# Moving the FFN's activation transposes from TensorE to SBUF transfers and VectorE block transposes

## The chip, the cores and the metric

The kernel runs on one core of a Trainium2 chip. The core has five engines that run side by side, each taking its own instructions in order: TensorE (PE; matrix products and transposes, results in PSUM), VectorE (DVE), ScalarE (ACT), GpSimd (POOL), and SyncE (SP), which here does nothing but issue transfers to the core's 16 DMA engines. They wait for one another by semaphores. The metric is the device time of one execution in microseconds (us); lower is better.

## What is computed

A transformer block in float32 over 2 x 1024 tokens of 1024 features: a layer norm, a convolution of width 3 that makes q, k and v, attention inside blocks of 128 tokens, two projections and a residual; then the part that matters here, an FFN with a gate over four experts:

```python
def ffn(x, ...):                                  # x: layer norm of the block's middle result
    y = einsum('bth,oh->bto', x, W_base) + b_base
    z = einsum('bth,erh->bter', x, lora_A[active])
    contribs = einsum('bter,eor->bteo', z, lora_B[active]) * 2.0
    logits = (einsum('bth,eh->bte', x, router_W) + router_b)[..., active]
    alpha = softmax(log(domain_prior[active] + 1e-12) + logits)
    return y + einsum('bteo,bte->bto', contribs, alpha)
x = x + attention(layernorm(x), ...)
x = x + ffn(layernorm(x), ...)
```

## The kernel before

**Stages.** The convolution runs first, then attention, then the FFN, which begins near 500 us and takes the rest. The FFN works on 16 tiles of 128 tokens, two tiles at a time: eight pairs, m = 0 to 7.

**One pair.** The product with W_base (1024 x 1024) is done in the Strassen-Winograd way. The pair's activations are a 2 x 2 grid of blocks, A11 and A12 for the first tile (features 0 to 511 and 512 to 1023), A21 and A22 for the second. From them come S1 = A21 + A22, S2 = S1 - A11, S3 = A11 - A21 and S4 = A12 - S2. Seven products of half size (`PRODUCTS`, line 1258) replace eight. Their order on TensorE is 1 (A11), 6 (S2), 2 (A12 with weight B21), 5 (S1), 7 (S3), 3 (S4 with weight B22), 4 (A22). For accuracy each operand is held as a high part (a rounding, made on ScalarE, `op_hi`, line 1248) and a low part (the rest, made on VectorE, `op_lo`, line 1251), and each product is three matmuls.

**Where the activations come from.** TensorE needs the features along the partitions, while the layer norm leaves the tokens there. For tile n: a load of the residual (`load_xr`, line 1169), an addition on GpSimd (`add_projb`, 1173), the attention's last projection on TensorE (`project`, 1176) and its addition (`residual`, 1187), statistics (`x_stats`, 1191), the reciprocal root on GpSimd (`x_rstd`, 1197) and the normalised tile on VectorE (`x_norm`, 1202). Then `transpose_x` (line 1208) transposes each half of the tile by four TensorE transposes of 128 x 128 into one PSUM bank. `op_hi`, `op_lo` and `sum_s` (line 1235) read that bank; A21 alone is first copied to SBUF by ScalarE (`keep_a21`, line 1232), since S1 and S3 would otherwise have two inputs in PSUM. `drop` (line 1254) frees a bank.

**Weights.** Four of the seven right-hand sides stay in SBUF, a fifth is kept too in pieces, and B21 and B22 are streamed in every pair as two loads of 1 MB each into the two `vh` buffers (`stream`, line 1634; `load_half`, line 1119). A `vh` buffer comes free when the product that read it has run: B22's halves take the buffers that product 2 has just read B21 from, and the next pair's B21 takes those of product 3.

**What sets the order.** A planner writes the order of every engine by hand before the program is built. Each piece of work is an `Op` (line 270) with an engine, an estimated time, a due time, the work it comes after and the buffers it takes (`need`) and returns (`give`). `trace` (line 293) simulates: when an engine is free, it takes, in order of due times, the first piece that is ready. What it writes down is an order; on the chip an engine then does its work in that order and waits for whatever is not yet there. DMA issues on SP are planned as one engine of this kind ("DMA"). Work with `port=True` is kept apart from GpSimd's work of the same kind. The buffer pool `a4` (11 buffers of 4 KB a partition) holds the normalised tiles, the operands and the sums; the pool `m` is the eight PSUM banks.

**The pair's loop** (line 1813): while pair m is multiplied, the two tiles of pair m+1 are projected, normalised and transposed: `plan_p(2m+3)`, product 1, `plan_p(2m+2)`, products 6 and 2, transposes of the second tile, product 5, the gate's small products (`z_products`), product 7, transposes of the first tile, products 3 and 4, with the gate's contributions (`experts`) in between. Pair 0's transposes lie before the loop.

Of the kernel before, what the change touches and what calls it, by code (L numbers as in the profile page):

```python
# [16 lines left out]
ALU = mybir.AluOpType  # L17
# [4 lines left out]
P = 128  # L22
# [17 lines left out]
def preln_block_kernel(  # L40
# [19 lines left out]
    nc = tc.nc  # L60
    N, L, D = x.shape
# [10 lines left out]
    E = lora_b.shape[0] // R  # L72
# [577 lines left out]
    DVE, ACT, PE, DMA = "DVE", "ACT", "PE", "DMA"  # L650
# [4 lines left out]
    loaded, gs, gone = {}, {}, {}  # L655
# [7 lines left out]
    at = [14.0]  # L663
# [3 lines left out]
    def turn(i, h):  # L667

        due = at[0]
        if h == 0:  # L670
            how = HOW[i]
            if how == "scalar":
                o = Op(ACT, 1.3, due - 8.0, 8.0, [loaded[i]], partial(ln_sum, i))
                o = Op(ACT, 1.2, due - 6.0, 8.0, [o], partial(ln_square, i))
                o = Op(DVE, 0.1, due - 4.5, 8.0, [o], partial(ln_variance, i), lag=1.8)
            else:
                lag = 1.0 if how == "vector" else 1.8
                o = Op(DVE, 1.6, due - 5.5, 8.0, [loaded[i]], partial(ln_stats, i), lag=lag)
# [52 lines left out]
    for q, (v, n, dc) in enumerate(units):  # L731
# [10 lines left out]
        o = Op(DVE, 1.28, due - 5.5, 9.0, took, partial(unit_sum, q))  # L742
        o = Op(ACT, 0.55, due - 3.5, 9.0, [o], partial(unit_hi, q))
        side = Op(DVE, 0.64, due - 1.5, 9.0, [o], partial(unit_lo, q))
        for i in range(2):
            d = dc + i
# [4 lines left out]
            for c in range(NCC):  # L751
                after = [last, side, ready[v, d]]
# [48 lines left out]
    for v, dc in [(v, dc) for v in (1, 2, 3) for dc in range(0, NDC, 2)] + [(4, 0), (4, 2)]:  # L801
        if (v, dc) == (2, 0):

            for r in range(4):
                load(
                    at[0] + r, 3.0, nc.sync.dma_start, mask[r::4], causal[ts(r, P // 4)],
                    after=[last],
# [4 lines left out]
        side = begin_step(v, dc, at[0])  # L812
# [18 lines left out]
    for c in range(NCC):  # L831
        got = load(
            at[0] - 4.0, 8.0, tokens_load, 0, c, t3, NV - 1,
            after=[gone["m", v, c] for v in (0, 5, 1, 2, 3)],
# [4 lines left out]
        o = Op(DVE, 2.7, at[0] + 1.0, 6.0, [got, gone[4, c]], partial(tokens_join, 0, c))  # L839
        o = Op(ACT, 0.6, at[0] + 4.0, 6.0, [o], partial(tokens_hi, 0, c))  # L840
# [23 lines left out]
    def a4(name, shape, dt=F32):  # L864
        return ap_.tile([P, *shape], dt, tag="a4", name=name, bufs=A4)
# [197 lines left out]
    NH = NDC // 2  # L1063
# [149 lines left out]
            xns.pop(g)  # L1213


    AT = {(0, 0): "A11", (0, 1): "A12", (1, 0): "A21", (1, 1): "A22"}

    def operand(m, n):
# [209 lines left out]
    gs = [ch * NB + b for ch in (2, 3, 0, 1) for b in range(NB)]  # L1428
    d = {}

    def pe(key, takes, after, f, lead=8.0, need=("m",), give=()):
        d[key] = Op(PE, takes, at[0], lead, [d.get(a) for a in after], f, need=need, give=give)
        at[0] += takes
        return d[key]

    def op(key, e, takes, due, after, f, lead=14.0, **kw):
        if e in (DVE, ACT):
            kw.setdefault("lag", LAG)
            takes *= ROOM
        d[key] = Op(e, takes, due, lead, [d[a] for a in after if a in d], f, **kw)  # L1440
        return d[key]
# [93 lines left out]
    def plan_p(n):  # L1535
        g = gs[n]
        ch = g // NB
        plan_x(n, at[0])

        if ch < NCHUNK - 2 and g % NB == 1:  # L1540
            for wc in range(NWC):
                op(("oh", ch, wc), DMA, 1.4, at[0] - 8.0, [("os", ch, wc)], partial(load_oh, ch, wc),
                   lag=3.0, need=("t4",), lead=6.0)
                d["ol", ch, wc] = d["oh", ch, wc]
        for h in range(2):
            pe(("P", n, h), MM,
               [("ol", ch, wc) for wc in range(NWC)] + [("rl", "pw", wc, h) for wc in range(NWC)],
               partial(project, g, h), give=("t4",) * 2 if h and g % NB == NB - 2 else ())
            op(("r", n, h, 0), DVE, 0.6, at[0] + 0.5, [("P", n, h), ("xb", n)],
               partial(residual, g, h), give=("m",))  # L1550
        op(("xs", n), DVE, 1.6, at[0] + 2.0, [("r", n, 0, 0), ("r", n, 1, 0)], partial(x_stats, g))
        op(("xp", n), POOL, 0.3, at[0] + 3.5, [("xs", n)], partial(x_rstd, g), lag=0.3)
        op(("xn", n), DVE, 0.75, at[0] + 5.0, [("xp", n)], partial(x_norm, g), need=("a4",), port=True)

    def plan_tx(m, t, h):

        n, o = 2 * m + t, AT[t, h]
        pe(("TX", n, h), 0.44, [("xn", n)], partial(transpose_x, gs[n], h), give=("a4",) if h else ())
        d["A", m, o] = d["TX", n, h]
        due = at[0]  # L1560

        def more(key, e, takes, dt, after, f, **kw):
# [12 lines left out]

        def done(n, dt, after):
            more(("x", n), DVE, 0.0, dt, after, partial(drop, m, n), give=("m",))

        def free(n, dt, after):
            more(("f", n), DVE, 0.0, dt, after, int, give=("a4",))  # L1580

        if {"A21", "A22"} <= made and ("s", m, "S1") not in d:
            more(("s", "S1"), DVE, 0.6, 1.9, [("c", "A21"), ("A", "A22")], partial(sum_s, m, "S1"))
            done("A22", 2.0, [("s", "S1"), ("l", "A22")])
            split("S1", 3.0, [])
        if {"A11", "A21", "A22"} <= made and ("s", m, "S2") not in d:
            more(("s", "S2"), DVE, 0.6, 2.6, [("s", "S1"), ("A", "A11")], partial(sum_s, m, "S2"),
                 need=("a4",))
            more(("s", "S3"), DVE, 0.6, 3.3, [("s", "S1"), ("A", "A11")], partial(sum_s, m, "S3"))
            done("A11", 3.4, [("s", "S2"), ("s", "S3"), ("l", "A11")])  # L1590
            split("S2", 4.0, [])
            split("S3", 6.0, [])
            free(0, 7.0, [("l", "S1"), ("l", "S3"), ("s", "S2")])
        if len(made) == 4:
            more(("s", "S4"), DVE, 0.6, 4.0, [("s", "S2"), ("A", "A12")], partial(sum_s, m, "S4"))
# [340 lines left out]
```

## Time and profile before

| | us |
|---|---|
| median of 3 runs | 753.68 (753.35 to 755.99) |
| the profiled execution, device time | 752.35 |
| its span in the profile | 750.5 |
| one pair in the loop, start to start | 30.3 |
| TensorE transposes `trx` (L1211), whole kernel, busy | 16.6, 128 of them |
| granted TensorE clock | 0.999 of full speed |

The span is the profiled execution without the 1.85 us around it. Busy time is counted per engine. A row of a group gives the line, engine, operation, what is written and read, the shape and the count, then the busy time, the mean time of one in ns, and the engine's idle time before it with what ended it. "PEq" or "SPq" is an engine's own queue: for SP, the row of a transfer is the time its issue holds SP, not the time the transfer takes.

The core's 16 DMA engines moved 149.46 MB in 65423 packets, 199 GB/s on the mean:

```profile
q1 hardware_dynamic: 61488, 138.51, 51.1%
```

That is the queue of SP: packets, MB and share of the 16 engines' span.

### The profile page before, as it was taken

How to read it: one execution, taken by the hardware profiler on the slowest of the kernel's cores; microseconds unless marked ns; L12 is line 12 of the kernel's file. 1: busy time of each engine (PE TensorE's matmuls, PEld its weight loads, DVE VectorE, ACT ScalarE, POOL GpSimd, SP SyncE). 2: the span in 40 equal slices, each digit the busy share in tenths (PEclk: the TensorE clock that was granted, in tenths of full speed). 3: DMA queues.
4: the chain of work that ended last, by engine and by line, in shares of the span. 5: the costliest groups of instructions: out<-in, count | busy, mean ns of one | idle time of the engine just before them, and what ended most of it. 6: DMA issues, size and time to landing. Idle time of an engine off the chain costs nothing.

```text
span 750.5 us, 12939 instructions
## 1 busy us (share of the span) xinstructions
PE 741.9 (99%) x4746; PEld 633.9 (84%) x4746; DVE 596.3 (79%) x1051; ACT 421.3 (56%) x1044; POOL 187.4 (25%) x154
## 2 busy tenths in 40 slices
PE   8999999999999999999999999999999999999997
PEld 7999988888888888888888888888888888888886
DVE  6888899889767898898888888599667677577752
ACT  6888336464745998798898789863212212212120
POOL 3224321310000223132222312454142251331401
PEclk9999999999999999999999999999999999999999
DMA  9936994995753113363245344797655566565644
GB/s 342 379 104 206 248 267 107 292 287 124 249 167 127 44 50 103 132 220 103 99 153 206 131 151 138 266 386 317 227 211 225 215 238 235 209 225 217 227 174 168
DMA packets 65423, 149.46 MB, mean 199 GB/s; under 512 B 5918, under 2 KB 25006, under 8 KB 60240
## 3 DMA queue, kind: packets, MB, share of 16 engines
q1 hardware_dynamic: 61488, 138.51, 51.1%
q0 software_dynamic: 3728, 10.00, 7.4%
q8 instruction: 37, 0.61, 0.3%
q14 instruction: 26, 0.21, 0.1%
q10 hardware_dynamic: 144, 0.13, 0.1%
HBM read 114.01 MB, written 34.60 MB: 198 GB/s over the span
## 4 chain that ended last, share of the span: by engine, by line
PE 95%; DVE 2%; DMA 1%; ACT 1%; SPq 1%; issue 0%; DVEq 0%; ACTq 0%
PE pm L141 27%; PE pq L141 11%; PE py_c L1271 6%; PE pw L141 6%; PE py_a L1271 6%; PE pp L141 6%; PE py_e L1271 6%; PE pv L141 5%; PE po L978 4%; PE s L914 4%; PE pt L961 4%; PE py_b L1271 3%; PE pz L1288 2%; PE trx L1211 2%; PE tr L393 1%; DMA xt<-in_x 1%
## 5 line engine op out<-in xcount | busy, mean ns | idle before, releaser
L141 PE MATMUL pm<-v,u 128*128 128x256 f32 (+1 forms) x1152 | 203.1, 337 | 1.2 <-ACT v L481 0.6
L141 PEld LDWEIGHTS pm<-v,u 128*128 128x128 f32 x1152 | 177.8, 189 | 24.0 <-ACT v L481 0.9
L954 POOL TENSOR_TENSOR p<-p,rs 128x1024 f32<-128x1024 f32 x32 | 60.7, 1908 | 250.4 <-DVE rs L950 240.5
L943 ACT ACTIVATE p<-p,nmx 128x128 f32<-128x128 f32 x256 | 99.7, 398 | 4.3 <-DVE nmx L938 4.1
L141 PE MATMUL pq<-yt,wqk 128*128 128x512 f32 x384 | 94.6, 398 | 0.0
L141 PEld LDWEIGHTS pq<-yt,wqk 128*128 128x128 f32 x384 | 70.3, 188 | 16.8 <-issue 1.9
L1174 POOL TENSOR_TENSOR xr<-xr,projb 128x1024 f32<-128x1024 f32 x16 | 38.8, 2426 | 113.2 <-DMA xr<-in_x 104.7
L943 ACT ACTIVATION_READ_ACCUMULATOR p<-p,nmx 128x1 f32 x256 | 50.2, 196 | 0.0
L929 DVE TENSOR_TENSOR p<-s,mask 128x512 f32<-128x512 f32 x64 | 42.4, 685 | 9.7 <-PE s L914 9.5
L141 PE MATMUL pw<-oT,wot 128*128 128x512 f32 x192 | 47.9, 397 | 0.0
L141 PE MATMUL pv<-wvt,yt 128*128 128x512 f32 x192 | 47.1, 395 | 0.0
L141 PEld LDWEIGHTS pv<-wvt,yt 128*128 128x128 f32 x192 | 36.0, 188 | 8.8
L141 PEld LDWEIGHTS pw<-oT,wot 128*128 128x128 f32 x192 | 35.9, 188 | 8.7 <-DVE oT L999 0.2
L431 POOL DMA_DIRECT2D g<-in_conv_w x24 | 21.3, 938 | 69.9 <-ACT g L427 36.2
L453 DVE TENSOR_TENSOR u<-g,u 128x768 fp32r<-128x768 f32 x40 | 37.5, 953 | 1.5 <-ACT u L449 1.4
L969 DVE COPY pT<-pt 128x512 f32<-128x512 f32 x32 | 21.8, 688 | 20.8 <-PE pt L961 20.8
L938 DVE TENSOR_REDUCE nmx<-p 128x8 f32<-128x1024 f32 x32 | 37.7, 1196 | 0.1
L1233 ACT COPY s<-trx 128x512 f32<-128x512 f32 x8 | 4.7, 588 | 56.9 <-PE trx L1211 56.9
L449 ACT CAST u<-g 128x768 fp32r<-128x768 f32 x40 | 32.7, 838 | 5.2 <-PE pm L141 4.8
L914 PEld LDWEIGHTS s<-qk,qk 64*128 64x128 f32 x512 | 30.1, 187 | 5.1 <-issue 2.3
L914 PE MATMUL s<-qk,qk 64*128 64x128 f32 x512 | 34.0, 280 | 0.0
L1369 ACT COPY u<-py_a 128x512 f32<-128x512 f32 x8 | 4.7, 588 | 51.9 <-PE py_a L1271 51.9
(206 smaller groups left out, 1532.6 us busy)
## 6 DMA issues: line engine op xcount, KB each, us to landing
wb_B<-wsd_B SPq DMA_DIRECT2D x32, 1024.0 KB, 7.1
g<-in_conv_w SPq DMA_DIRECT2D x48, 384.0 KB, 8.3
mdr<-m SPq DMA_DIRECT2D x36, 256.0 KB, 3.0
g<-in_conv_w POOLq DMA_DIRECT2D x24, 384.0 KB, 7.3
xt<-in_x SPq DMA_DIRECT2D x16, 512.0 KB, 9.8
xr<-in_x SPq DMA_DIRECT2D x16, 512.0 KB, 5.6
out<-xr SPq DMA_DIRECT2D x14, 512.0 KB, 6.5
ml<-mdr SPq DMA_DIRECT2D x18, 384.0 KB, 4.0
```

What stands on the lines that cost most here:

```text
L141: nc.tensor.matmul(ps, l[a], r[b], start=first and i == 0, stop=last and i == 2)
L449: nc.scalar.copy(us[v, dc][0], raws[v, dc])
L453: nc.vector.tensor_tensor(lo, raws.pop((v, dc)), hi, ALU.subtract)
L914: nc.tensor.matmul(s[j][:, b, :], qh[ts(j, DH), ts(b, P)], kh[ts(j, DH), ts(b, P)], start=True, stop=True,)
L929: nc.vector.tensor_tensor(ps[i][0][:, ts(j, NB), :], ss[i][j], mask[:, None, :].to_broadcast([P, NB, P]), ALU.add,)
L938: nc.vector.tensor_reduce(nmx, p, AX.X, ALU.max, negate=True)
L943: nc.scalar.activation(p[:, k, :], p[:, k, :], AF.Exp, bias=nmx[:, k : k + 1], accum_out=sm[:, k : k + 1],)
L954: nc.gpsimd.tensor_tensor(p, p, rs[:, :, None].to_broadcast([P, 2 * NB, P]), ALU.mult)
L961: nc.tensor.transpose(pt[:, ts(b, P)], ps[i][0][:, j * NB + b, :], ident)
L978: nc.tensor.matmul(po[ts(j, DH), ts(b, P)], vh[:, b, ds((i % 4) * P + j * DH, DH)], pT[:, j, ts(b, P)], start=True, stop=True,)
L1174: nc.gpsimd.tensor_tensor(xrs[g], xrs[g], pwt["b"], ALU.add)
L1271: nc.tensor.matmul(pys[m, b], l[x], r[y], start=opens and c == 0 and i == 0, stop=c == NH - 1 and i == 2, skip_group_check=not opens,)
```

## The change

For pairs 1 to 7, the transposes leave TensorE. A tile is instead rearranged in SBUF: `spread` issues 16 transfers on SP, in four groups (a = 0 to 3) of four (q = 0 to 3). Each moves, for 32 tokens and all eight chunks of 128 features, a run of 32 features (128 bytes) per chunk from the tokens' 32 partitions to partitions 32a to 32a+31. After it the tile consists of 32 x 32 blocks that each lie where they belong but are not transposed. `turn` transposes these blocks on VectorE, 128 x 512 elements in one instruction for each half of the tile, and writes them back into the normalised tile. The result therefore stands in SBUF and not in PSUM, so A21 needs no copy, the sums and low parts of these pairs read two SBUF inputs and are planned with `port=True`, and buffers of `a4` are held in place of PSUM banks. In the plan a group of four transfers costs 0.7 us of SP (`XD`), and its data is taken to be there 4.0 us after the group's end. The last product of the last pair also gets two further conditions for its order. Pair 0 keeps its transposes on TensorE.

```diff
+    QB = P // 32
+    xps = {}
+
+    def spread(g, a):
+        if a == 0:
+            xps[g] = a4(f"xp_{g}", (D,))
+        src = xns[g].rearrange("p (c a f) -> p c a f", a=QB, f=32)
+        dst = xps[g].rearrange("p (c q f) -> p c q f", q=QB, f=32)
+        for q in range(QB):
+            nc.sync.dma_start(dst[ts(a, 32), :, q], src[ts(q, 32), :, a])
+
+    def turn(g, h):
+
+        t = xns[g][:, ts(h, 512)]
+        nc.vector.transpose(t, xps[g][:, ts(h, 512)])
+        trxs[g, h] = t.rearrange("p (c j) -> p c j", c=NH)
+        if h == 1:
+            xns.pop(g)
+            xps.pop(g)
...
     def sum_s(m, n):
         g0, g1 = gs[2 * m : 2 * m + 2]
+        a21 = trxs[g1, 0] if (g1, 0) in trxs else s_of(m, "S3")
         a, b, how = {
-            "S1": (trxs.get((g1, 1)), s_of(m, "S3"), ALU.add),
+            "S1": (trxs.get((g1, 1)), a21, ALU.add),
             "S2": (s_of(m, "S1"), trxs.get((g0, 0)), ALU.subtract),
-            "S3": (trxs.get((g0, 0)), s_of(m, "S3"), ALU.subtract),
+            "S3": (trxs.get((g0, 0)), a21, ALU.subtract),
...
+    XD = 0.7
...
         op(("xn", n), DVE, 0.75, at[0] + 5.0, [("xp", n)], partial(x_norm, g), need=("a4",), port=True)
+        if n > 1:
+            for a in range(QB):
+                op(("xd", n, a), DMA, XD, at[0] + 2.5 + XD * a, [("xn", n), ("xd", n, 0)], partial(spread, g, a),
+                   lag=4.0 if a else 0.0, need=("a4",) if a == 0 else ())
...
-        pe(("TX", n, h), 0.44, [("xn", n)], partial(transpose_x, gs[n], h), give=("a4",) if h else ())
+        if m == 0:
+            pe(("TX", n, h), 0.44, [("xn", n)], partial(transpose_x, gs[n], h), give=("a4",) if h else ())
+        else:
+            op(("TX", n, h), DVE, 0.6, at[0] - 1.5 + 0.7 * h, [("xd", n, a) for a in range(QB)],
+               partial(turn, gs[n], h), give=("a4",) if h else ())
...
-        if o == "A21":
+        if o == "A21" and side:
+            d["c", m, o] = d["A", m, o]
+        elif o == "A21":
...
-            more(("l", o), DVE, 0.6, 1.2, [("h", o)], partial(op_lo, m, o))
+            more(("l", o), DVE, 0.6, 1.2, [("h", o)], partial(op_lo, m, o), port=side)
...
-            more(("s", "S3"), DVE, 0.6, 3.3, [("s", "S1"), ("A", "A11")], partial(sum_s, m, "S3"))
+            more(("s", "S3"), DVE, 0.6, 3.3, [("s", "S1"), ("A", "A11")], partial(sum_s, m, "S3"),
+                 port=side)
...
-        pe(("Y", m, 3, 1 + x), 6 * 0.12, [("wl", "B22", 1, m)], partial(multiply_last, m, x), need=())
+        pe(("Y", m, 3, 1 + x), 6 * 0.12, [("wl", "B22", 1, m), ("E", m, 0, 1), ("Y", m, 3, x)], partial(multiply_last, m, x), need=())
```

More of the change, by code (lines that the diff above doesn't have):

```diff
@@ L1553, in plan_p @@
         op(("xn", n), DVE, 0.75, at[0] + 5.0, [("xp", n)], partial(x_norm, g), need=("a4",), port=True)
+        if n > 1:
+            for a in range(QB):
+                op(("xd", n, a), DMA, XD, at[0] + 2.5 + XD * a, [("xn", n), ("xd", n, 0)], partial(spread, g, a),
+                   lag=4.0 if a else 0.0, need=("a4",) if a == 0 else ())
     def plan_tx(m, t, h):
         n, o = 2 * m + t, AT[t, h]
-        pe(("TX", n, h), 0.44, [("xn", n)], partial(transpose_x, gs[n], h), give=("a4",) if h else ())
+        if m == 0:
[3 more added lines that the diff above has]
+               partial(turn, gs[n], h), give=("a4",) if h else ())
         d["A", m, o] = d["TX", n, h]
         due = at[0]
+        side = m > 0
         def more(key, e, takes, dt, after, f, **kw):
             op((key[0], m, *key[1:]), e, takes, due + dt, [(a[0], m, *a[1:]) for a in after], f, **kw)
-        if o == "A21":
+        if o == "A21" and side:
+            d["c", m, o] = d["A", m, o]
+        elif o == "A21":
             more(("c", o), ACT, 0.5, 0.5, [("A", o)], partial(keep_a21, m), need=("a4",), give=("m",))
@@ L1576, in done @@
         def done(n, dt, after):
-            more(("x", n), DVE, 0.0, dt, after, partial(drop, m, n), give=("m",))
+            both = ("x", m, {"A11": "A12", "A12": "A11"}.get(n)) in d
+            give = ("m",) if not side else ("a4",) if both else ()
+            more(("x", n), DVE, 0.0, dt, after, partial(drop, m, n), give=give)
         def free(n, dt, after):
@@ L1582, in plan_tx @@
         if {"A21", "A22"} <= made and ("s", m, "S1") not in d:
-            more(("s", "S1"), DVE, 0.6, 1.9, [("c", "A21"), ("A", "A22")], partial(sum_s, m, "S1"))
+            more(("s", "S1"), DVE, 0.6, 1.9, [("c", "A21"), ("A", "A22")], partial(sum_s, m, "S1"),
+                 need=("a4",) if side else (), port=side)
             done("A22", 2.0, [("s", "S1"), ("l", "A22")])
@@ L1587, in plan_tx @@
             more(("s", "S2"), DVE, 0.6, 2.6, [("s", "S1"), ("A", "A11")], partial(sum_s, m, "S2"),
-                 need=("a4",))
-            more(("s", "S3"), DVE, 0.6, 3.3, [("s", "S1"), ("A", "A11")], partial(sum_s, m, "S3"))
+                 need=("a4",), port=side)
+            more(("s", "S3"), DVE, 0.6, 3.3, [("s", "S1"), ("A", "A11")], partial(sum_s, m, "S3"),
+                 port=side)
+            if side:
+                more(("x", "A21"), DVE, 0.0, 3.4, [("s", "S3"), ("x", "A22")], partial(drop, m, "A21"),
+                     give=("a4",))
             done("A11", 3.4, [("s", "S2"), ("s", "S3"), ("l", "A11")])
@@ L1594, in plan_tx @@
         if len(made) == 4:
-            more(("s", "S4"), DVE, 0.6, 4.0, [("s", "S2"), ("A", "A12")], partial(sum_s, m, "S4"))
+            more(("s", "S4"), DVE, 0.6, 4.0, [("s", "S2"), ("A", "A12")], partial(sum_s, m, "S4"),
+                 port=side)
             done("A12", 4.1, [("s", "S4"), ("l", "A12")])
```

## The prediction

> **What bounds the kernel now.** First the page's busy times and its chain of waits.
>
> ```profile
> PE 741.9 (99%) x4746; PEld 633.9 (84%) x4746; DVE 596.3 (79%) x1051; ACT 421.3 (56%) x1044; POOL 187.4 (25%) x154
> PE 95%; DVE 2%; DMA 1%; ACT 1%; SPq 1%; issue 0%; DVEq 0%; ACTq 0%
> ```
>
> TensorE is busy 99% of the span and carries 95% of the chain that ended last. Time taken off TensorE is time gained, as long as everything TensorE needs still comes in time. So I then read one FFN pair on TensorE as a timeline (start us, length us, what).
>
> ```profile
> 552.29 2.94 PE L1271 MATMUL py_a<-wb_B,A 128*128 128x512 f32 x12
> 555.07 1.03 PE L1211 MATMUL trx<-identr,xn 128*128 128x128 f32 x8
> 555.86 3.05 PE L1271 MATMUL py_e<-wb_wr,S 128*128 128x512 f32 x12
> ...
> 564.05 1.03 PE L1211 MATMUL trx<-identr,xn 128*128 128x128 f32 x8
> 564.84 2.98 PE L1271 MATMUL py_e<-wb_B,S 128*128 128x512 f32 x12
> ```
>
> A merged row's length overlaps the next row, so I take start to start: 555.86 - 555.07 = 0.79 us for the eight transposes of a tile, and 0.79 again for the other tile. Nothing is idle around them.
>
> **What is removed.** Pairs 1 to 7 lose their transposes: 7 x 2 x 0.79 = **11.06 us** of TensorE. ScalarE also loses the copy of A21 (L1233, 0.59 us a pair), which hides under ScalarE's 6 us in 30. Pair 0 keeps its transposes. With nothing late, the profiled execution goes from 752.35 to 741.3 us. The median of the runs shown is 753.68, 1.33 above the profiled execution; that makes 742.6.
>
> **What is added on SP.** Each later tile costs 16 transfers of 32 KB in runs of 128 B, so 32 a pair. The pair now issues about 8 on SP. The rows that price an issue:
>
> ```profile
> L530 SPq DMA_DIRECT2D mdr<-m x36: 319/327/1681, 60.4 to 230.7; - x36
> 585.92 0.90 SPq L1034 DMA_DIRECT2D oht<-ohd  x2
> ```
>
> A store out of SBUF holds SP 0.33 us (minimum/median/maximum in ns), and the trace leaves about 0.04 between two: 0.37. Two loads back to back took 0.90: 0.45 each. No row goes from SBUF to SBUF, so I take 0.41 of 0.37 to 0.49: 16 x 0.41 = **6.6 us of SP for a tile**, 13 of 28.8 us for a pair. The plan books 4 x 0.7 = 2.8. Here a rule speaks for the change: the Trainium skill's "DMA: Bandwidth & Descriptors" (Issuing engines are not separate DMA queues) calls the sequencer's issue time usually small relative to the DMA itself. By the rule a tile costs its transfer. By the row, the issue is twice the transfer, as the next sum shows. I follow the row.
>
> **What is added on the DMA engines.** A tile is 4096 runs. The trace's packet records give medians of 27 ns for 512 B, 46 for 1024 B and 84 for 2048 B: a line of 8.5 ns plus 0.037 ns a byte, hence 13 ns for 128 B, 4096 x 13 / 16 = 3.4 us a tile. The same page asks for 512 B at least for full rate, because shorter writes are read, changed and written back (Specifications), and says elsewhere (Why small descriptors are slow) that SBUF to SBUF escapes the penalty. Priced like a 512 B packet, a tile is 6.9 us. I take 13 ns, the line through the rows, and keep 27 for the range. Room for it, by windows (length, busy us and count of PE, PEld, DVE, ACT, POOL, clock, DMA share, GB/s):
>
> ```profile
> 541.30:571.70 30.40, 30.40 (x168) 25.38 (x167) 21.75 (x44) 5.88 (x12) 9.47 (x6) 1.00 0.55 204
> 632.40:662.70 30.30, 30.30 (x168) 25.27 (x167) 21.68 (x44) 5.88 (x12) 9.47 (x6) 1.00 0.65 243
> ```
>
> DMA is busy 16.7 to 19.7 us of a pair; plus 2 x 3.4 that is 23.5 to 26.5 of 28.8 us. It fits, narrowly.
>
> **What is added on VectorE.** Four block transposes a pair. No row shows one; the nearest are its 128x512 operations, 0.68 us: +2.7 on 21.7 = 24.4 us. They can't cost nothing, since each reads and writes 512 elements a lane; 1.2 us each, a 128x1024 row, is the upper end. And seven operations a pair (three low parts, four sums) change from a PSUM input to two SBUF inputs:
>
> ```profile
> L1252 DVE TENSOR_TENSOR S<-s,S 128x512 fp32r<-128x512 f32 x32 | 32.0, 1018 | 0.2
> L1252 DVE TENSOR_TENSOR A<-trx,A 128x512 fp32r<-128x512 f32 x24 | 15.8, 685 | 1.8 <-ACT A L1249 1.8
> 633.94 2.37 DVE L1252 TENSOR_TENSOR S<-s,S 128x512 fp32r<-128x512 f32 x1
> ```
>
> The same subtraction costs 685 ns from PSUM and a mean of 1018 from SBUF, because once a pair it is held (2.37 us at 633.94, while GpSimd's addition runs from 633.36 for 2.40). I allow one more such hold, 1.7 us, a pair.
>
> **What this makes late.** I count t from the start of a pair (541.25, 602.1, 632.4 and so on), and look for the supply with the least slack. It is B22's weights, two loads of 1 MB: their buffers come free when product 2 has used B21, and product 3 needs them.
>
> ```profile
> 614.55 12.93 SPq L1123 DMA_DIRECT2D wb_B<-wsd_B  x3
> ...
> L1123 SPq DMA_DIRECT2D wb_B<-wsd_B x1: 327/327/327, 614.5 to 614.5; - x1
> DMA to landing us min/median/max: 4.9/4.9/4.9
> ...
> L1123 SPq DMA_DIRECT2D wb_B<-wsd_B x1: 320/320/320, 615.9 to 615.9; - x1
> DMA to landing us min/median/max: 7.3/7.3/7.3
> ```
>
> Issued at t = 12.45 and 13.8, the halves land at 17.3 and 21.1 (614.5 + 4.9 and 615.9 + 7.3, less 602.1). Product 3 starts its second half at t = 24.9 now, and at 23.3 once both groups of transposes are gone. SP issues in the plan's order. In it the first tile's transfers have due times near 5 to 7 and B22's loads near 16 and 17, so whatever is ready goes ahead of B22. The tile is ready when x_norm (L1204) ends:
>
> ```profile
> 551.84 0.81 DVE L1204 TENSOR_SCALAR xn<-xr,lnmv_b,lnrs_b 128x1024 f32<-128x1024 f32 x1
> 639.80 0.82 DVE L1204 TENSOR_SCALAR xn<-xr,lnmv_b,lnrs_b 128x1024 f32<-128x1024 f32 x1 [0.67 <-POOL lnrs_b L1199]
> ```
>
> - **The pairs from 541 and 572**: x_norm ends at t = 11.4. SP is taken until 18.0, B22 goes out at 18.0 and 18.4. Two megabytes queued together land in 4.9 + about 3 us (1 MB at some 350 GB/s), so at 25.9: product 3 stands 2.6 us. Twice: 5.2.
> - **The four pairs from 602 on**: x_norm ends at t = 8.2 before. But VectorE's queue grows. The second tile's transfers go out behind B22 (about 18.4 to 25) and land by 27, so its sums start near 27.4 instead of 24.9, in a pair 1.6 shorter, with 1.4 of transposes more; some 2.1 us of other additions fill the gap. Net the queue in front of x_norm is 3.3 us longer, and 1.7 with the held operation: 5.0 if TensorE never stood. A stall s gives VectorE that much back, so s = 8.2 + 5.0 - s + 14.5 - 23.3 = 4.4 - s, thus 2.2 each: 8.8.
> - **The pair from 511**: both x_norms are early (end at t = 9.1 and 14), so the second tile's transfers can get ahead of B22's second half. Behind all 32, B22 lands near 28.4, 5.1 late; behind one tile, 0.9. I take 3.0.
>
> A11 itself survives: landed by 27, transposed 27.7, split by 29.8, needed at 31.5.
>
> **The sum.** -11.06 + 5.2 + 8.8 + 3.0 = +5.9 us: 752.35 to 758.3 profiled, **759.6** against the median. With 0.37 an issue, SP is free 0.6 earlier and all stalls together shrink by about 4; with 0.49 they grow by 8: own range 755 to 768.
>
> **Rivals.**
> - **The cover holds (faster).** If an issue costs 0.33 with no gap, or VectorE's queue stays short because the waiting time takes it up, the later four pairs have B22 at 8.2 + 5.3 + 0.4 + 7.9 = 21.8, in time, and the two POOL-bound pairs stand 1.3 each. -11.06 + 2.6 + 1 = -7.5: 746; with no stall at all, 742.6. For it: DMA stands idle some 4 us before B22 goes out, and VectorE has gaps of 2 to 3 us a pair. Against it: SP issues in order.
> - **Short packets at 27 ns (slower still).** This decides above some 18 ns. Then DMA needs 17 to 20 + 13.8 = 31 to 33 us in a pair of 28.8. The second tile lands near 33 instead of 27, A11 is split near 35.5, 4 us late: 7 x (4 - 1.58) = +17, 771. For it: the 512 B rule; against it: the straight line of the packet times.
> - **The change does less than it says**: an eleventh buffer (a4) may be short, so transfers wait in the plan. Then VectorE, not TensorE, sets a pair, and the time lies between the forecast and the last rival.
>
> **Chances.** Forecast 0.40, faster rival 0.37, short packets 0.15, the rest 0.08. A measurement of this kernel tells 0.5% (3.8 us) from no change. Of the forecast's range about a quarter, and a little of the faster rival's, lies inside that: faster 0.38, same 0.14, slower 0.48. The range 743 to 776 reaches both rivals.
>
> **What would show it.** Line 1211 falls from 128 to 16. SP's issues of 32 KB: 0.41 us each, 16 in 6.6. TensorE's gap in front of py_e's second half of product 3, put down to wb_B, about 2 us a pair. The time to landing of the 32 KB transfers near 2 us, and their packets near 13 ns. VectorE's x_norm of the first tile near t = 11. It is wrong if TensorE has no gaps before product 3 (then 742 to 746), if the gaps stand before product 1 (A11, the second tile), or if the packets take 27 ns.

## The result and the profile after

The changed kernel takes **828.86 us** (median of 4 runs, 826.24 to 831.62) against 753.54 for the kernel before on the same chip (4 runs, 753.35 to 755.99): a ratio of 1.0992, 95% interval 1.0949 to 1.1035. The profiled execution took 828.31 us, its span 826.5. A pair lasts 40.7 us where it lasted 30.3. One execution of e18_nothing_behind, further down, was in a slower state (816.6 us), and the times given for it leave that one out.

First the page of the kernel after: the busy times, and the chain of waits that ended last by engine.

```profile
PE 751.3 (91%) x4634; PEld 633.1 (77%) x4634; DVE 615.3 (74%) x1079; ACT 419.4 (51%) x1037; POOL 189.5 (23%) x154
PE 67%; SPq 12%; DVE 8%; DMA 8%; issue 2%; ACT 1%; POOL 0%; DVEq 0%; ACTq 0%
```

TensorE lost its 112 transposes (4746 to 4634 instructions), but its busy time rose from 741.9 to 751.3 us, although 11.06 us of work left it: 730.8 were due, so the rest of its work takes 20.5 us more. Its idle time went from 8.6 us (750.5 - 741.9) to 75.2 (826.5 - 751.3), 66.6 more. These are all of it: -11.1 + 20.5 + 66.6 = 76.0 = 826.5 - 750.5. SP's issues were 1% of the chain and are 12%.

The transfers and the block transposes, by their lines (the transfers: ns minimum/median/maximum; the transposes: busy us, mean ns, idle time before):

```profile
L1227 SPq DMA_DIRECT2D xp<-xn x224: 585/609/1541, 520.0 to 792.9; - x112
L1232 DVE STREAM_TRANSPOSE xn<-xp 128x512 f32<-128x512 f32 x28 | 18.5, 693 | 93.3 <-DMA xp<-xn 93.3
```

An issue holds SP 0.61 us, and the next starts 0.65 us after it. A block transpose takes 0.69 us. The packets of 128 B took 13 ns each.

Now SP's own queue in the pair that begins at 629.0, and TensorE in the same pair (start us, length us, what; in brackets the idle time before and what ended it):

```profile
644.31 0.33 SPq L1123 DMA_DIRECT2D wb_B<-wsd_B  x1
645.82 10.98 SPq L1227 DMA_DIRECT2D xp<-xn  x16
656.90 0.54 SPq L1123 DMA_DIRECT2D wb_B<-wsd_B  x1
657.54 10.42 SPq L1227 DMA_DIRECT2D xp<-xn  x16
668.00 0.60 SPq L1171 DMA_DIRECT2D xr<-in_x  x1
668.70 0.85 SPq L1123 DMA_DIRECT2D wb_B<-wsd_B  x2
```

```profile
653.61 1.53 PE L1295 MATMUL py_e<-wb_B,S 128*128 128x512 f32 x6
662.17 2.93 PE L1295 MATMUL py_e<-wb_B,S 128*128 128x512 f32 x6 [7.03 <-DMA wb_B<-wsd_B]
664.90 3.18 PE L1295 MATMUL py_c<-wb_wr,A 128*128 128x512 f32 x12
```

The first half of B22 goes out at 644.31. In the kernel before, the second half followed 1.35 us later; here a whole tile's 16 transfers stand in front of it, it goes out at 656.90, and TensorE stands 7.03 us for it. After the other tile's 16 transfers come the next pair's residual and B21. And the six matmuls behind the gap take 2.93 us, where the same six took 1.53 right before it. The stretch of this pair (length; busy us and count of PE, PEld, DVE, ACT, POOL; clock; DMA share; GB/s) has the clock at 0.87, where it was 1.00 before:

```profile
629.00:669.70 40.70, 32.97 (x153) 26.38 (x154) 23.43 (x45) 4.78 (x10) 9.89 (x6) 0.87 0.63 189
```

The waits in the FFN, from 500 to 830 us (total, times, longest), here the largest and those of TensorE:

```profile
POOL xr L1174 <- DMA xr<-in_x: 161.1, 11, 27.3
DVE xn L1232 <- DMA xp<-xn: 93.3, 14, 8.4
...
PE py_e L1295 <- DMA wb_B<-wsd_B: 34.2, 7, 7.5
...
PE pp L141 <- DMA oht<-ohd: 15.4, 3, 13.6
PE py_a L1295 <- ACT A L1273: 13.5, 1, 13.5
```

TensorE's three large waits make 63.1 of its 75.2 idle us, and two of them are loads that SP issued late. They do not fall in the same pairs. B22's two halves are split by a block of 16 transfers in three pairs (from 601, 644 and 727), and TensorE stands 7.0 to 7.5 us for the second half. In two pairs both halves go out together ahead of all 32 transfers (683.32 and 767.04). There TensorE does not wait for B22 at all, but 13.6 us for oht and 13.5 for A, at the end of the 32, and these pairs are no shorter.

### The profile page after: what moved, and what is told of

Read it like the earlier page. It is cut to its first block, busy times and chain, and to the rows that moved or that the text cites. A ratio compares the mean times of both kernels' runs of the same rounds, so it can differ in the third digit from the quotient of the medians.

```text
span 826.5 us, 13082 instructions
## 1 busy us (share of the span) xinstructions
PE 751.3 (91%) x4634; PEld 633.1 (77%) x4634; DVE 615.3 (74%) x1079; ACT 419.4 (51%) x1037; POOL 189.5 (23%) x154
## 4 chain that ended last, share of the span: by engine, by line
PE 67%; SPq 12%; DVE 8%; DMA 8%; issue 2%; ACT 1%; POOL 0%; DVEq 0%; ACTq 0%
PE pm L141 24%; SPq L1227 12%; PE pq L141 10%; DMA wb_B<-wsd_B 6%; PE pw L141 5%; PE pv L141 5%; PE po L978 4%; PE s L914 3%; PE pp L141 3%; PE pt L961 3%; PE py_a L1295 3%; PE py_b L1295 2%; DVE S L1276 1%; PE tr L393 1%; PE py_c L1295 1%
## 5 line engine op out<-in xcount | busy, mean ns | idle before, releaser
L141 PEld LDWEIGHTS pm<-v,u 128*128 128x128 f32 x1152 | 177.7, 189 | 24.5 <-DVE v L486 1.0
L1232 DVE STREAM_TRANSPOSE xn<-xp 128x512 f32<-128x512 f32 x28 | 18.5, 693 | 93.3 <-DMA xp<-xn 93.3
L141 PEld LDWEIGHTS pq<-yt,wqk 128*128 128x128 f32 x384 | 70.4, 188 | 16.8 <-issue 1.5
L1295 PE MATMUL py_e<-wb_B,S 128*128 128x512 f32 x90 | 32.2, 512 | 34.2 <-DMA wb_B<-wsd_B 34.2
L1295 PEld LDWEIGHTS py_e<-wb_B,S 128*128 128x128 f32 x90 | 21.8, 251 | 42.4 <-DMA wb_B<-wsd_B 25.3
L1273 ACT CAST A<-xn 128x512 fp32r<-128x512 f32 x21 | 12.9, 619 | 67.5 <-DVE xn L1232 47.7
L1324 ACT COPY zk<-pz 72x256 f32<-72x256 f32 x8 | 2.9, 368 | 80.0 <-PE pz L1312 80.0
L141 PE MATMUL pp<-pw,oht 128*128 128x512 f32 x96 | 27.4, 434 | 15.4 <-DMA oht<-ohd 15.4
L1295 PE MATMUL py_a<-wb,A 128*128 128x512 f32 x96 | 27.0, 431 | 15.7 <-ACT A L1273 13.5
```

The costliest lines, as they stand in the source:

```text
L141: nc.tensor.matmul(ps, l[a], r[b], start=first and i == 0, stop=last and i == 2)
L1295: nc.tensor.matmul(pys[m, b], l[x], r[y], start=opens and c == 0 and i == 0, stop=c == NH - 1 and i == 2, skip_group_check=not opens,)
```

## The experiments

All times are medians; ratios are to the kernel before in runs of the same chip.

### Is it the number of issues, or what each transfer is like?

**e4_no_transfers**: `turn` transposes blocks of the tile itself; nothing is moved.

```diff
-        for q in range(QB):
-            nc.sync.dma_start(dst[ts(a, 32), :, q], src[ts(q, 32), :, a])
...
-        t = xns[g][:, ts(h, 512)]
-        nc.vector.transpose(t, xps[g][:, ts(h, 512)])
+        t = xps[g][:, ts(h, 512)]
+        nc.vector.transpose(t, xns[g][:, ts(h, 512)])
```

> The 224 transfers are left out; VectorE transposes the 32 by 32 blocks of the normalised tile straight into the second buffer, so that the features are not where the products want them. The plan's order and all of VectorE's work stay. Theory A and rival C: with the transfers gone TensorE is the bound again without its 112 transposes, 741 to 748. Rival V: VectorE keeps its load, so 780 or more.

Measured: 748.44 us (747.76 to 749.48), ratio 0.9925 (0.9904 to 0.9946). Five of its seven pairs take 28.6 us, and TensorE waits 4.9 us in the whole FFN. So VectorE's part is hidden but for these waits, and the loss, 80 us against this run, comes with the transfers.

**e2_long_runs**: the same 16 transfers of 32 KB a tile, but one run of 1 KB a partition instead of eight of 128 B.

```diff
-            nc.sync.dma_start(dst[ts(a, 32), :, q], src[ts(q, 32), :, a])
+            nc.sync.dma_start(xps[g][ts(a, 32), ts(q, 256)], xns[g][ts(q, 32), ts(a, 256)])
```

> The same 16 transfers a tile, of the same 32 KB, between the same groups of 32 partitions, but each partition's 1024 bytes in one run instead of eight of 128 bytes; the features then lie elsewhere, so the products are not those of the reference. If the issue's price goes by the runs, an issue falls from 0.61 to 0.32 to 0.42 us and the time to 745 to 775, with theory A. If the price is that of any SBUF to SBUF transfer of 32 partitions, it stays 0.61 and the time 820 to 830. Rival C: the packets are an eighth in number (46 ns each instead of 13), so 760 or less even if the issue stays at 0.61.

**e5_wide**: 16 transfers a tile of 32 KB, each over all 128 partitions instead of 32.

```diff
-            nc.sync.dma_start(dst[ts(a, 32), :, q], src[ts(q, 32), :, a])
+            k = a * QB + q
+            dst, src = (t[g].rearrange("p (b k f) -> p k b f", k=16, f=32)[:, k] for t in (xps, xns))
+            nc.sync.dma_start(dst, src)
```

> The same 16 transfers a tile, 32 KB each in 256 runs of 128 bytes, but each goes over all 128 partitions (two runs a partition) and stays in its partitions, so the features are not where the products want them. Bytes, packets and order stay. Theory A1, the price of an issue goes by the 32 partitions (the four loads of 32 partitions into mask cost 0.61 us in the trace of the kernel before as well): an issue falls to 0.32 to 0.42 us, and the prediction's own sum, made with 0.41, is tested: 750 to 770. Theory A2, the price is that of any transfer from SBUF to SBUF: it stays at 0.6 and the time at 815 to 830.

Measured: 823.77 (1.0924, 1.0859 to 1.099) and 830.80 (1.1022, 1.0978 to 1.1067). The issues by their lines, of the first and of the second:

```profile
L1227 SPq DMA_DIRECT2D xp<-xn x224: 507/588/1549, 522.5 to 789.1; - x112
```

```profile
L1229 SPq DMA_DIRECT2D xp<-xn x224: 593/619/1907, 521.0 to 796.6; - x112
```

Neither the length of the runs nor the number of partitions sets the price or the time. It is 0.59 to 0.62 us for each of these transfers of 32 KB from SBUF to SBUF; no run has another size.

**e1_two_queues**: the odd transfers go out from ScalarE.

```diff
-            nc.sync.dma_start(dst[ts(a, 32), :, q], src[ts(q, 32), :, a])
+            (nc.sync, nc.scalar)[q % 2].dma_start(dst[ts(a, 32), :, q], src[ts(q, 32), :, a])
```

> Half of the 224 short-run transfers are issued by ScalarE instead of SP (q odd), nothing else changes. Theory A, SP's issue time: 32 issues of 0.655 us (0.61 and a gap of 0.045) hold SP 21 us a pair, and with half of them elsewhere SP is held 10.5 us; the pair falls from 40.75 us to 29 to 33, the time to 745 to 775. Rival C, the short packets (their number or landing) set the pair: the packets stay the same, so 820 to 830. Rival V, VectorE (28 more instructions, two SBUF inputs held by GpSimd) sets it: 820 to 830.

Measured: 789.66 (788.2 to 791.12), ratio 1.0472 (1.0394 to 1.0549); TensorE's wait for B22 falls from 34.2 to 8.6 us. Half of SP's issues away gives half of the loss back. It is not a clean half: ScalarE's own work stands behind its transfers (its wait of 41.2 us at `zk`), and SP stands 32.2 us in 12 waits for the landing of a load of B21 or B22 (why is said at e18).

**e6_second_tile** and **e7_first_tile**: only the second tile of each later pair (A21 and A22, whose transfers go out first) goes the new way, or only the first; the other keeps its transposes on TensorE. The diff is of e6 (e7 has 0 for 1, and keeps ScalarE's copy of A21).

```diff
-        if n > 1:
+        if n > 1 and n % 2 == 1:
             for a in range(QB):
...
-        if m == 0:
+        if m == 0 or t != 1:
...
-        side = m > 0
+        side = m > 0 and t == 1
```

> Only the second tile of each later pair (A21, A22, the one whose transfers are issued ahead of B22's loads) goes the new way; the first stays on TensorE. SP is held 10.5 us a pair. If B22 behind the transfers is what costs: the tile is ready at t = 8, SP is free at 18.7, B22 lands near 26.6 where 24.1 is wanted, 2.5 us a pair less 0.79 saved: 760 to 772. If the two tiles together are needed to make SP late: 747 to 755.

> Only the first tile of each later pair (A11, A12, whose transfers are issued behind B22's loads) goes the new way. If B22 is what costs, it goes out in time and the pair loses no more than A11's lateness (SP free near 29, landed 31, split 33.5, wanted at 32.3): 748 to 762, faster than with the second tile alone. If VectorE's queue, which stands at the transposes of this tile until the transfers land, is what costs: slower than with the second tile alone, 770 or more.

Measured: 776.91 (1.0316, 1.0286 to 1.0346) and 787.11 (1.0448, 1.041 to 1.0487). With the second tile TensorE waits 18.8 us for B22, 3.5 at most; with the first it waits for A (11.0) and for x_norm (9.0) and not for B22. The two losses against the kernel before, 23 and 34 us, make 57 of the 75: 16 issues a pair are too many already, and the second 16 cost no less.

### Is it the plan?

**e3_plan_price** books a group of four transfers at its true price; **e11_plan_queue** does that too, and books the weights' loads at the time of their issue only.

```diff
-    XD = 0.7
+    XD = 2.6
```

```diff
-            op(("wl", w, h, m), DMA, 2.75,
+            op(("wl", w, h, m), DMA, 0.4,
...
-               partial(load_half, w, h), lead=30.0, lag=2.0, need=("vh",))
+               partial(load_half, w, h), lead=30.0, lag=5.5, need=("vh",))
```

> The plan books 2.6 us for a group of four transfers instead of 0.7; the work stays the same, only the order written down changes. Rival D, the order (the weights B22 stand behind transfers that the plan took for cheap): with an order that knows the price, PE's waits for wb_B (59 us with those of its loads of weights in the trace) mostly go, and the time is 780 or less. Theory A: SP is held for 21 us a pair as before, so at least 800.

> The plan is given the measured queue: a group of four transfers 2.6 us of SP, a load of B21 or B22 0.4 us with 5.5 us to its landing (before: 0.7 and 2.75 with 2.0). Only the order changes. Theory D, the order alone is wrong: 775 or less. Theory L: each tile's chain of 10.5 us of issues and a landing stays, but the pairs may overlap better: 785 to 825.

Measured: 830.43 (1.1013, 1.0945 to 1.108) and 838.09 (1.1119, 1.1076 to 1.1162). With the true price the plan puts B22 better, and TensorE waits elsewhere instead (waits of e3 from 500 to 829 us):

```profile
PE py_e L1295 <- DMA wb_B<-wsd_B: 20.2, 8, 3.9
PE py_e L1295 <- ACT S L1273: 13.5, 6, 4.8
PE py_a L1295 <- ACT A L1273: 10.5, 5, 2.1
```

A better order of the same issues is not to be had this way. The wrong `XD` explains where the blocks stand, not that they cost.

### What behind the transfers carries the loss?

**e9_b22_scalar**: B22's loads from ScalarE's queue.

```diff
-        nc.sync.dma_start(wb[n, h].bitcast(F32), wsd[n, h])
+        (nc.scalar if n == "B22" else nc.sync).dma_start(wb[n, h].bitcast(F32), wsd[n, h])
```

> B22's loads are issued by ScalarE, so they no longer stand behind the short-run transfers on SP; all else as in the changed kernel. Theory B, B22 behind SP's queue is what costs (the stall that the prediction worked with): PE's waits for wb_B go and the time falls to 775 or less. Theory L, a loop sets the pair: 16 issues (10.5 us), 16 more (10.5), landing (2), and some 17 us on VectorE and GpSimd from the block transposes, where VectorE stands until the transfers land, to the next pair's first normalised tile, 40 us in all: the pair stays at 36 to 41 us and the time at 795 to 830.

Measured: 840.74 (1.1154, 1.1126 to 1.1183). TensorE no longer waits for B22; from 560 to 800 us it now waits 20.5 us for oht. B22's wait, which the prediction rested on, is not the only limit (that ScalarE now issues loads is a change too, see e18).

**e12_not_waited**: the 224 transfers read the residual tile, and VectorE transposes without waiting for them.

```diff
-        src = xns[g].rearrange("p (c a f) -> p c a f", a=QB, f=32)
+        src = xrs[g].rearrange("p (c a f) -> p c a f", a=QB, f=32)
...
-        nc.vector.transpose(t, xps[g][:, ts(h, 512)])
+        nc.vector.transpose(t, xrs[g][:, ts(h, 512)])
```

> The 224 transfers are issued as in the changed kernel, with the residual tile as their source, but nobody waits for what they write: VectorE transposes the residual tile's blocks straight away, so that the products' operands are not the reference's. SP keeps its 21 us a pair and B22 its place behind the transfers; VectorE no longer stands. Theory B, with 0.655 an issue in the prediction's sum (SP free at 8 to 11 + 10.5, B22 landed 8 later, 4 to 6 us late a pair): 770 to 790. Theory L: without the landing and VectorE's standing the loop is broken, so most of the 75 us goes: 785 or less. Both give less than 790; what is above it belongs to SP alone.

Measured: 815.89 (1.0824, 1.0797 to 1.0852). The 93.3 us that VectorE stood for the transfers are worth 13 of the 75.

From here my theory was a loop: the next pair's residual goes out only behind both blocks, so landing, addition, norm and the next block follow one another. **e13_loads_gpsimd** takes the residual's and oht's loads to GpSimd, **e14_loads_scalar** to ScalarE, **e15_all_loads** both of them and B21 and B22 to ScalarE.

```diff
-        nc.sync.dma_start(oht[ch, wc].bitcast(F32), ohd[ch][wc])
+        nc.gpsimd.dma_start(oht[ch, wc].bitcast(F32), ohd[ch][wc])
...
-        nc.sync.dma_start(xrs[g], xr_of[g])
+        nc.gpsimd.dma_start(xrs[g], xr_of[g])
```

> The residual loads xr (L1171) and the oht loads (L1034) are issued by GpSimd instead of SP; the transfers and the weights' loads stay on SP. Theory of the loop (the next pair's residual is issued only behind both blocks of 16 transfers, so transfers, landing, addition, norm and transfers again follow one another): the loads no longer stand behind 22 us of issues, the pair falls from 40.7 to 33 to 36 us, the wait of GpSimd's addition for xr falls from 161 to under 80 us, and the time is 775 to 800. Rival (what counts is only that SP is held, by way of B22 and B21; late residuals are a symptom): the pair stays at 39 us or more, 815 to 835.

> The same two loads are issued by ScalarE instead of SP. Theory of the loop: about as when GpSimd issues them, 775 to 805, somewhat more if a load that waits for its buffer holds ScalarE's high parts. Rival: 815 to 840, with the pair at 39 us or more.

> Residual, oht, B21 and B22 are all issued by ScalarE; in the FFN only the transfers and the output's stores are left on SP. Theory of the loop with B22 as a second cost: nothing but the transfers stands behind the transfers, so the pair falls below that of the kernel with the residual's and oht's loads alone moved, to 31 to 34 us, 755 to 785. Against it: B22's loads alone on ScalarE had made the kernel slower (840.7), because a load that waits for its buffer holds ScalarE; if that decides, the time is 800 or more, and TensorE's waits are put down to ScalarE's high parts (A, S).

Measured: 832.54 (1.1056, 1.103 to 1.1083), 829.01 (1.1011, 1.0966 to 1.1056) and 861.04 (1.1413, 1.1377 to 1.1449). The theory of that one loop falls: in e13 GpSimd's wait for the residual did fall, from 129 to 36 us between 560 and 800, and nothing came of it. In that stretch VectorE waited 85.7 us for transfers and TensorE 33.9 for B22.

So I cut the chain and the loads together. **e16_issue_alone**: the transfers read the projection's bias, so SP waits for no x_norm, and nobody waits for the transfers. **e17_issue_and_loads**: that, and the residual's and oht's loads on GpSimd as in e13. **e18_nothing_behind**: that, and B22 on ScalarE as in e9.

```diff
-        src = xns[g].rearrange("p (c a f) -> p c a f", a=QB, f=32)
+        src = pwt["b"].rearrange("p (c a f) -> p c a f", a=QB, f=32)
...
-        nc.vector.transpose(t, xps[g][:, ts(h, 512)])
+        nc.vector.transpose(t, xrs[g][:, ts(h, 512)])
```

> The 224 transfers stay where they are in SP's order, but read the projection's bias, which is always there, and VectorE transposes blocks of the residual tile without waiting for them: SP never waits for x_norm, nothing waits for a transfer, and what is left is the time that SP's issues take in front of the other loads (the values are not the reference's). If SP's time in front of the loads makes the loss by itself: about as slow as with the residual as the transfers' source (815.9), 800 or more. If it takes the chain x_norm, 16 issues, landing, blocks, operands as well, in a loop with the next pair's x_norm: SP's 24.5 us a pair fit into 30, the pair falls to 31 to 34 us, and the time is 755 to 785.

> The same, and the residual's and oht's loads issued by GpSimd, so that only B21, B22 and the output's stores are still behind the transfers (the values are not the reference's). If the residual's and oht's loads carry what the run before has left: 750 to 765. If they carry nothing: the same time as the run before, within 5 us.

> As in the run before (transfers that read the projection's bias and that nobody waits for; the residual's and oht's loads on GpSimd), and B22's loads issued by ScalarE, where they had gone out 0.85 us apart without holding it; B21 and the stores of the output stay on SP (the values are not the reference's). If the loss is the sum of parallel loops through SP's queue, of which B22 between and behind the blocks is the last: TensorE's 7 to 8 us gap before the second half of product 3 goes, with the slowed matmuls behind it, the pair falls from 39 to 29 to 32 us, and the time is 750 to 770. If the 224 transfers cost time in another way (DMA engines, SBUF, VectorE's and GpSimd's shared access): 795 or more, with waits of TensorE that are not put down to wb_B.

Measured: 815.16 (1.084, 1.0802 to 1.0877), 811.82 (1.0773, 1.0747 to 1.0799) and 809.43 (1.071, 1.0651 to 1.0768). The first says most: transfers that nobody waits for, and that wait for no data, cost 67 us against the kernel without them (815.16 - 748.44). What is left of them is SP's time in front of other issues, with 17.6 us in which SP waited for landings of earlier transfers and 11.2 us for a buffer (waits that the profile puts down to VectorE and TensorE), and what they take of the DMA engines. In e17 a pair can be followed to the end; TensorE there:

```profile
617.80 2.93 PE L1295 MATMUL py_e<-wb_B,S 128*128 128x512 f32 x6 [7.86 <-DMA wb_B<-wsd_B]
620.52 3.81 PE L1295 MATMUL py_c<-wb_wr,A 128*128 128x512 f32 x12
...
656.37 2.93 PE L1295 MATMUL py_e<-wb_B,S 128*128 128x512 f32 x6 [6.99 <-DMA wb_B<-wsd_B]
```

From the end of one gap to the end of the next are 38.6 us (656.37 - 617.80). Full work is 28.6 (e4's pair), the gap 7.0, a wait for ScalarE 0.5, and the matmuls behind the first gap take 1.4 more (six in 2.93 for 1.53) and 0.9 more (twelve in 3.81 for 2.96 in e4): 38.4 of the 38.6. In this pair of e17, then, B22's second half behind a block is nearly all that is left. But with B22 taken out as well the time hardly moved (2.4 us), TensorE waited for B21 (24.5 us from 500 on) and for VectorE's additions (17.8), and SP's queue in e18 shows why:

```profile
592.53 1.03 SPq L1123 DMA_DIRECT2D wb_B<-wsd_B  x2
...
595.93 34.45 SPq L1227 DMA_DIRECT2D xp<-projb  x32
630.48 1.02 SPq L1123 DMA_DIRECT2D wb_B<-wsd_B  x2
```

32 issues now stretch over 34.45 us instead of some 21, and B21 and the stores wait for their end: SP is taken for the whole pair of 38 us. Between the issues at 598.05 and 614.82 only six others went out. The DMA engines are full there (busy share 0.98 from 598 to 604 us, 1.05 from 604 to 610), and a transfer took up to 16.9 us to land, at a median of 2.0. In the program as built, SP's and ScalarE's transfers take eight semaphores in turn, and each waits for the landing of the one eight before it. So a slow load holds up the burst behind it: from 500 us on, SP stood 76.7 us at these transfers for landings of earlier ones in e18 (45.3 of it for loads of B21 or B22), 17.6 in e16, and only 8.8 in the kernel after, where this is no large part of the loss. What e18 would take without these waits no run shows. It also means that e1, e9, e14, e15 and e18, which put transfers or loads on ScalarE's queue, test more than their place.

### Fewer issues

**e8_dram** stores a tile to DRAM in one transfer and reads it back in four, in runs of 1 KB. x_norm writes the features in the order that makes these runs whole.

```diff
+    def stash(g):
+        xqd[g] = dram.tile([P, D], F32, name=f"xqd_{g}")
+        nc.sync.dma_start(xqd[g], xns[g])
...
-        for q in range(QB):
-            nc.sync.dma_start(dst[ts(a, 32), :, q], src[ts(q, 32), :, a])
+        src = xqd[g].rearrange("(q i) (a e) -> a i q e", q=QB, a=QB)[a]
+        dst = xps[g][ts(a, 32)].rearrange("p (q e) -> p q e", q=QB)
+        nc.sync.dma_start(dst, src)
```

**e10_dram_second** does this for the second tile only; the first keeps its transposes on TensorE.

> Both tiles of each later pair, but through DRAM: the normalised tile is written with its features in another order, stored by one transfer of 128 partitions and loaded by four of 32 partitions in runs of 1 KB, so 5 issues a tile instead of 16: 0.35 + 4 x 0.655 = 3.0 us of SP. Theory A: with SP held 6 us a pair instead of 21 the time falls to 745 to 762. Rival C, bytes and landing: each pair moves 1 MB more than with transfers inside SBUF and has two landings in a row, so 775 or more if these set the pair.

> Only the second tile of each later pair goes through DRAM (one store, four loads), the first stays on TensorE. TensorE saves 7 x 0.79 = 5.5 us. SP is held 3 us a pair, nothing that stands in front of the next pair's first product waits for a transfer. 747 to 752 if both theories hold; 755 or more if VectorE's work with two SBUF inputs already delays TensorE.

Measured: 763.23 (1.0125, 1.0089 to 1.0161) and **747.72** (746.34 to 748.81), ratio 0.9914 (0.9892 to 0.9936). The second is faster than both kernels; against the one before the gain is 0.9%. The loads' issues in e8, and the busy times and chain of e10's page:

```profile
L1233 SPq DMA_DIRECT2D xp<-xqd x56: 302/431/1757, 524.1 to 729.6; - x56
```

```profile
PE 735.9 (99%) x4690; PEld 627.4 (84%) x4690; DVE 602.7 (81%) x1065; ACT 419.5 (56%) x1037; POOL 188.8 (25%) x154
PE 88%; DVE 6%; DMA 2%; ACT 2%; issue 1%; SPq 1%; POOL 0%; DVEq 0%; ACTq 0%
```

A load from DRAM holds SP 0.43 us, a tile has 5 issues for 16, and twice the bytes go through the DMA engines. In e10 TensorE is busy 99% again.

Put in order of SP's issues for the rearrangement, in one pair:

| issues a pair on SP | kernel | us |
|---|---|---|
| 0 | e4 | 748.4 |
| 5 | e10 (one tile) | 747.7 |
| 10 | e8 | 763.2 |
| 16 | e6, e7 (one tile) | 776.9, 787.1 |
| 16, and 16 on ScalarE | e1 | 789.7 |
| 32 | after, e2, e5 | 828.9, 823.8, 830.8 |

## Why the prediction was wrong

**The direction was right, the size was not**: +5.9 us were forecast, +75 came, outside the range.

- **The price of an issue is the first step that failed.** It was taken between a store (0.37) and a load (0.45) as 0.41 us, 6.6 us a tile, from rows that have DRAM at one end. It is 0.65 start to start, 10.4 to 13.0 us a tile (the longer ones hold a wait for a landing, or a slow issue). In the prediction's own sum 10.4 us a tile makes 2 x 6.4 + 4 x 4.1 + 8.7 - 11.06 = +27 us, some 780 us in all (an estimate). So the price alone does not make the 75. A row of before shows that an issue can cost this much:

```profile
L653 SPq DMA_DIRECT2D mask<-in_causal x4: 564/610/650, 105.8 to 134.6; - x4
```

  It is a load of 32 partitions early in the kernel, so it shows no rule, but it lies above the upper end of 0.49 that I gave to an operation without a row.
- **The second failed step is where the search for late supplies ended.** "I look for the supply with the least slack" took B22 alone and priced only its stall, 2.2 to 3.0 us a pair. The wait is there, at that instruction, but as 7.0 to 7.5 us. B22's halves were thought to go out together behind one tile. In three pairs the plan put a block between them, and in the one from 629 the second half went out at t = 27.9 (656.90 - 629.0) instead of 18.4. Behind B22 in SP's order are the next pair's residual and oht loads and B21; the prediction never named them. Of TensorE's waits, oht has 15.4 us, 13.6 of it in one of the two pairs in which B22 is in time.
- **"A11 itself survives"** holds for most pairs, not all: TensorE waited once for A, 13.5 us, in the other of these two pairs. The argument was for one tile's transfers in 6.6 us.
- **x_norm near t = 11**: in the pair from 629 the transfers that go first start at 16.8, since the projection that feeds it had itself waited for oht.
- **Nothing was allowed for the matmuls after a gap.** TensorE's work takes 20.5 us more. The kernel before, with 8.6 us of idle time in all and a mean clock of 0.999, has no row that shows it. Three stretches of the pair from 629 do (columns as above): the gap's first 3.40 us, its rest with the first matmuls behind it, and what follows.

```profile
655.14:658.54 3.40, 0.00 (x0) 0.00 (x0) 0.21 (x1) 0.00 (x0) 0.00 (x0) 1.00 0.48 63
658.54:665.37 6.83, 3.20 (x8) 2.52 (x9) 3.43 (x12) 1.24 (x2) 0.00 (x0) 0.50 0.68 190
665.37:669.70 4.33, 4.33 (x21) 3.49 (x20) 0.11 (x1) 0.37 (x1) 0.00 (x0) 1.00 0.39 68
```

  The granted clock is halved 3.40 us into the gap and is full again 3.20 us after the matmuls have begun (2.93 us for six, against 1.53 before the gap). In the whole FFN TensorE worked 39.5 us at a clock of 0.50, which is 19.8 us more than at full clock: nearly all of the 20.5. The Trainium skill's "TensorE: Matmul & The Clock Gate" (Part 1) says that the array falls to half its clock after an idle window of about 3.4 us, and needs as long a busy one to come back; the trace agrees.
- **Right**: 11.06 us leave TensorE (L1211 keeps 16 transposes), though only 5.7 come back in the time even without transfers (e4: 0.75% of 754); packets of 13 ns on the straight line, so the rival of short packets falls; block transposes of 0.69 us (0.68 taken); landing about 2 us; VectorE's additions hidden. The Trainium skill's "DMA: Bandwidth & Descriptors" (Issuing engines are not separate DMA queues) calls issue time usually small beside the transfer; the row was followed rightly against it, and was still too low: 16 issues held SP 10.4 us, and their packets take 3.4 us of the 16 engines.

**What is shown and what stays open.** Shown: the loss comes with the transfers and not with VectorE's work (e4). It does not follow the runs, the partitions or the order in the plan (e2, e5, e3, e11), nor the bytes (e8 moves twice as many and loses 10 us). It grows with the number of issues on SP (the table), and most of it is there without anyone waiting for the data (e16). Not settled: how it divides among B22, B21, oht, the residual and the operands. Each one taken out alone gave 13 us, nothing, or lost time (e12, e14, e9, e13), and the two chains cut together gave 17 (e17). These paths limit at about the same length, so removing one shows the next. That reading fits all of these runs, and the two pairs of the kernel after in which B22 is in time. But none of the runs removes all of the paths cleanly, since in e18 SP waited for landings instead.

## What to carry to other kernels

Count the issues that a change puts on a queue, price one by a row of the same kind, and if there is none, take the worst row that the trace has. Then list everything that stands behind them in that queue, loads for the next round too, and not only the supply with the least slack: a queue that issues in order delays them all, and giving one of them another queue only shows the next. When a rearrangement is wanted, fewer and larger transfers matter more than fewer bytes: 5 issues through DRAM beat 16 inside SBUF here.

## What the runs showed of the hardware

- An issue of a 32 KB transfer from SBUF to SBUF holds SP 0.59 to 0.62 us (median), for runs of 128 B and of 1 KB, over 32 and over 128 partitions. Stores of a tile to DRAM took 0.32 and loads from DRAM 0.43 in e8, but the mask's four loads from DRAM 0.61 in the kernel before. So the memories at the ends do not settle the price, and what does is open.
- Two queues issued such transfers side by side at nearly the pace of one: in e1 the starts that nothing held up lay 0.65 us apart on SP and 0.66 on ScalarE (medians), 0.65 with SP alone.
- A lone gap of 7 us costs TensorE more than the gap: the matmuls behind it ran at a granted clock of 0.50 for 3.20 us.
